# A graph network's attention units: the last column block of the probabilities turned by VectorE and the DMA queues in place of TensorE

## The chip, the cores and the metric

The kernel runs on one core of one Trainium2 chip. The metric is the device time of one execution in microseconds. The kernel before took 2339.39 us, the median of three runs (2338.75 to 2340.38). The profile comes from a further execution of 2340.76 us.

## The reference

A batch of 32 graphs with 512 nodes and 64 features each passes through four layers. All four share one 512 x 512 adjacency matrix, symmetric and scaled on both sides by the root of the node's degree. Each layer normalises its input, applies a ReLU, computes an update and adds it to the input. The first three layers are a neighbour sum, two plain graph convolutions, and an additive attention. The fourth, in which most of the time is spent, has eight heads of dot-product attention and an output attention over what the heads produce:

```python
def gat_layer(x, graph, W, b):
    h = x @ W
    s = jnp.einsum('bnd,bmd->bnm', h, h) * graph
    s = jnp.where(s == 0.0, NEG_INF, s)
    a = jax.nn.softmax(s, axis=2)
    return jnp.einsum('bnm,bmd->bnd', a, h) + b
heads = jax.vmap(lambda W, b: gat_layer(flow_x, graph, W, b))(Wh, bh)
...
x = jax.nn.leaky_relu(cat, negative_slope=0.01)
out = gat_layer(x, graph, W_out, b_out)
return jax.nn.leaky_relu(out, negative_slope=0.01)
```

For every graph this is nine attentions with a 512 x 512 score matrix each: scores, a masked softmax along the rows, and the product of the probabilities with the values.

## The kernel before

The file holds two forms: a general one (L1133 on), which did not run here, and the fast one (`fast_form`, L23), which did. All data are float32. With P = 128 partitions, N = 512 nodes make C = 4 row blocks and 4 column blocks.

**Two stages.** The first stage (L756 to L1105) computes the first three layers, for pairs of graphs. The second stage (L1110 to L1129), from about 470 us to the end, computes the fourth layer. The change lies in the second, apart from the helper that prepares the heads' features.

**Units.** The second stage is a row of 144 units. A unit is a pair of attentions that lie in the two halves of the 128 partitions (`halves(k)`, L206, k = 0 or 1, 64 rows each). A `Heads` unit (L457) is two heads of one graph, four such units for each graph, 128 in all. An `Out` unit (L549) is the output attention of two graphs, 16 in all. Both derive from `Pair` (L313).

**Slots.** Time is cut into slots of which each unit starts four, one for each row block r; the next unit starts in the fifth. `planned` (L649) makes a function `slot(k)` (L665), which emits what each unit does in slot k; `at(k, off, span)` (L652) yields the units whose slot number, counted from their own start, is off to off + span - 1, and the step in it. TensorE, VectorE and ScalarE get their instructions exactly in the order in which the code emits them (`manual_schedule`, L121), so the order in `slot` is each engine's queue. Counted from the unit's start, a unit does this:

- Slots -1 to 2: `scores(r)` (L381) on TensorE, two matmuls (k = 0 and 1) into `s_ps`, at the head of the slot. Two `s_ps` tiles exist.
- Slots 0 to 3: `soft(r)` (L357). VectorE adds the mask `flow_neg`, negates and takes the row's extreme in one instruction for each k (L372); ScalarE takes the exponential and the row sum (L365) into `p_att`. Between the second L372 and what follows, the code calls `mid()` (L699), which holds the division of an earlier unit.
- Slots 5 to 8 (`TR` = 5, L299): `transpose(j)` (L391) for column block j = 0 to 3. Sixteen TensorE transposes of 64 x 128 (L399), which alternate between the two row halves of the source, fill two PSUM tiles `pt_ps`; ScalarE copies one of them (L405) and VectorE the other (L407) into `pt_att`. VectorE's copy is emitted after the slot's `soft` and `mid`.
- Slots 6 to 9 (`VA` = 6): `values(j)` (L409). For each k one matmul of 512 columns (L414), accumulated over j in the one tile `av`, which holds the two halves k in the partitions 0 to 63 and 64 to 127.
- Slot 5: `recips()` (L419): VectorE inverts the row sums (L424) and turns them (L426), SP writes them to DRAM (`rec_row`, four small DMAs, L429) and reads them back as a row spread over 64 partitions (`recb`, two DMAs, L434).
- Slot 9 (`END`, L301): `normalize()` (L441), the division: `o_att` = `av` x `recb` (L443), emitted in `mid()`.
- Slots 10 to 13: the heads' weights (`y_ps`, L526), the activation (`cat`, L534 and L311), or for an `Out` unit the bias, a transpose back and the output DMA (L614). The products of an `Out` unit (`gT_ps`, L565) are spread over eight slots before it starts.

In slots where the `y_ps` or `g_ps` matmuls run first (`row_halves`, L499; "led" in the code), the transposes are emitted after the values, otherwise before them.

PSUM: `ps_m` has three tiles with one tag (L1116), which `pt_ps`, `y_ps`, `g_ps`, `gT_ps`, `gV_ps`, `hx_ps` and `back_ps` share.

**What the change touches beside it.** `Heads.prep_late` (L469), six slots before the first unit of a graph: VectorE makes the normalised features `hn` (L474, L475) and the least value for a later test (L478), then GpSimd makes `hs`, the features times `root_d`, once for each k (L483). In the next slot TensorE transposes `hs` into `hx_ps` (L290), and ScalarE copies it (L292). `Out.prep_late` (L580), at the end of the slot two before the unit starts: VectorE makes `gs` = `gT` x `urow` (L583), which the next slot's scores read, and a reduction for the test (L584).

The pools: `wk` has two buffers for each name unless one is given (L1112), `dram` three (L1113), `p_att` and `pt_att` two each.

Of the kernel before, what the change touches and what calls it, by code (L numbers as in the profile page):

```python
# [8 lines left out]
F32 = mybir.dt.float32  # L9
AF = mybir.ActivationFunctionType  # L10
OP = mybir.AluOpType
# [3 lines left out]
P = 128  # L15
# [7 lines left out]
def fast_form(  # L23
# [25 lines left out]
    nc = tc.nc  # L49
    B, N, F = x.shape  # L50
    C = N // P
    H, _, D = w_heads.shape
    G = min(8, B)
    NG = B // G
    F2 = 2 * F

    const = ctx.enter_context(tc.tile_pool(name="const", bufs=1))
    xpool = ctx.enter_context(tc.tile_pool(name="xpool", bufs=1))
# [12 lines left out]
    early = ctx.enter_context(tc.tile_pool(name="early", bufs=1))  # L71
# [17 lines left out]
    def load_blockdiag(src, name):  # L89
        t = setup.tile([P, F2], F32, name=name)  # L90
        nc.vector.memset(t, 0.0)
        for k in range(2):
            nc.gpsimd.dma_start(t[k * F : (k + 1) * F, k * F : (k + 1) * F], src)
        return t
# [19 lines left out]
    for k in range(2):  # L114
        rows = slice(k * F, (k + 1) * F)
# [45 lines left out]
    root_d = const.tile([P, C], F32, name="root_d")  # L161
    urow = const.tile([P, N], F32, name="urow")
# [43 lines left out]
    def halves(k):  # L206
        return slice(k * F, (k + 1) * F)
# [8 lines left out]
    def acc(name, shape):  # L216
        return acc_of[0].tile(shape, F32, name=name, tag=acc_of[1])
# [22 lines left out]
    def gat_weights():  # L240
        pw = acc("wgT_ps", [P, F2])
        nc.tensor.transpose(pw, wg2, ident)
# [56 lines left out]
    TR = C + 1  # L299
# [13 lines left out]
    class Pair:  # L313
# [19 lines left out]
        def prep_late(self, step):  # L333
            pass


        def make_v(self):
            pass


# [40 lines left out]
        def scores(self, r):  # L381
# [3 lines left out]
            for k in range(2):  # L385
# [2 lines left out]
                    start=True, stop=True,  # L388
                )

        def transpose(self, j):  # L391
            pt = pbuf.tile([P, 2, N], F32, name="pt_att", bufs=2)
            self.pts[j] = [pt[:, k] for k in range(2)]

            ps = [ps_m.tile([P, 2, C, F], F32, name="pt_ps", tag="m") for half in range(2)]
            for k in range(2):
                for r in range(C):
                    for half in range(2):
                        nc.tensor.transpose(  # L399
                            ps[half][:, k, r],  # L400
                            self.p[halves(half), k, r, j * P : (j + 1) * P],
                            ident[halves(half), halves(half)],
                        )
            pth = pt.rearrange("p k (r half q) -> p k r half q", r=C, half=2)
            nc.scalar.copy(pth[:, :, :, 0, :], ps[0])  # L405

            return lambda: nc.vector.tensor_copy(pth[:, :, :, 1, :], ps[1])  # L407

        def values(self, j):  # L409
            pt = self.pts.pop(j)  # L410
            if j == 0:
                self.av = ps_v.tile([P, N], F32, name="av")
            for k in range(2):
                nc.tensor.matmul(  # L414
                    self.av[halves(k), :], lhsT=self.v(k, j), rhs=pt[k],
                    start=(j == 0), stop=(j == C - 1),
                )

        def recips(self):  # L419

# [36 lines left out]
    class Heads(Pair):  # L457
# [3 lines left out]
        hs = {}  # L461
# [7 lines left out]
        def prep_late(self, step):  # L469
            b = self.b  # L470
            if step == -2 and self.i == 0:
                mean, rstd = (t[:, b % 2, :, None].to_broadcast([P, C, F]) for t in flow_stats[b // 2])
                h = early.tile([P, C, F], F32, name="hn3", bufs=3)
                nc.vector.tensor_tensor(h, xs[b // G][:, b % G], mean, OP.subtract)  # L474
                nc.vector.scalar_tensor_tensor(  # L475
                    h, h, 0.0, rstd, op0=OP.max, op1=OP.mult
                )
                nc.vector.tensor_reduce(  # L478
                    least[:, b * C : (b + 1) * C], h, AX.X, OP.max
                )  # L480
                hs = early.tile([P, C, 2, F], F32, name="hs3", bufs=2)
                for k in range(2):
                    nc.gpsimd.tensor_tensor(  # L483
                        hs[:, :, k, :], h, root_d[:, :, None].to_broadcast([P, C, F]), OP.mult
                    )
                Heads.hs[b] = hs
                Heads.hn[b] = h

# [60 lines left out]
    class Out(Pair):  # L549
# [23 lines left out]
        def make_v(self):  # L573
# [3 lines left out]
            self.gV = wk.tile([P, C, P], F32, name="gV", bufs=1)  # L577
            nc.scalar.copy(self.gV, ps)

        def prep_late(self, step):  # L580
            if step == 2:
                self.gs = wk.tile([P, N], F32, name="gs", bufs=1)
                nc.vector.tensor_tensor(self.gs, self.gT, urow, OP.mult)  # L583
                nc.vector.tensor_reduce(  # L584
                    least_out[:, self.b // 2 : self.b // 2 + 1], self.gT, AX.X, OP.min,
                    apply_absolute_value=True,
                )
# [61 lines left out]
    def planned(units, products):  # L649
        units = units + [None] * 4  # L650

        def at(k, off, span=C):  # L652

            for u in range(len(units)):
                if units[u] and 0 <= k - u * C - off < span:
                    yield units[u], k - u * C - off

        exps = []

        def led_in(k):  # L660
            for u, j in at(k, -3 * C, 3 * C + END + 5):
                if u.leads(j - 3 * C):
                    yield u, j - 3 * C

        def slot(k):  # L665
            for u, r in at(k, -1):
                u.scores(r)

            led = list(led_in(k))
            for u, off in led:
                u.row_halves(off)

            while exps:
                exps.pop(0)()

            copies = []

            def transposes():  # L680
                for u, j in at(k, TR):
                    copies.append(u.transpose(j))

            if not led:
                transposes()
            for u, j in at(k, VA):
                u.values(j)
            for u, j in at(k, VA - 1, 1):
                u.make_v()
            for n, u in products:  # L690
                u.product(k - n * C)
            for u, j in at(k, -3 * C, 3 * C):
                u.prep_pe(j - 2 * C)
            if led:
                transposes()
            for u, j in at(k, END, 5):
                u.end_pe(j)

            def mid():  # L699
                for u, j in at(k, END, 1):  # L700
                    u.normalize()

            now = list(at(k, 0))
            for u, r in now:
                exps.append(u.soft(r, mid))
            if not list(led_in(k + 1)):
                while exps:
                    exps.pop(0)()
            if not now:
                mid()  # L710
            for copy in copies:
                copy()
            for u, j in at(k, END, 5):
                u.end_late(j)
            for u, j in at(k, TR, 1):
                u.recips()
            for u, j in at(k, -3 * C, 3 * C):
                u.prep_late(j - 2 * C)

        return slot  # L720
# [34 lines left out]
    with (  # L755
# [47 lines left out]
        class Spread:  # L803
# [169 lines left out]
        def slot(k, more):  # L973
# [158 lines left out]
def general_form(  # L1132
# [27 lines left out]
    NG = B // G  # L1160
    F2 = 2 * F

# [66 lines left out]

    wgT2 = const.tile([P, F2], F32, name="wgT2")  # L1230
    bh = const.tile([P, H], F32, name="bh")
# [459 lines left out]
```

## Time and profile before

| | |
|---|---|
| median of three runs | 2339.39 us |
| the profiled execution | 2340.76 us |
| its span in the trace | 2338.9 us |
| mean granted TensorE clock | 0.986 |
| L399 transposes | 9216, 415.6 us busy |
| L405 and L407 copies | 576 each, 582 and 687 ns |
| L414 value matmuls | 2304 passes, 618 to 625 ns each, in overlapping pairs |
| L483 `hs` on GpSimd | 64 instructions of 128 x 256, idle otherwise |
| DMA, whole kernel | 53.11 MB, 23 GB/s on average |

How to read it: "busy" is the time in which at least one instruction of the engine was running, PE is TensorE's matmuls and PEld its weight loads, DVE is VectorE, ACT ScalarE, POOL GpSimd, SP the engine that issues DMAs. A row of instructions names the line of the code, the engine, the tile written and the tiles read (out<-in), the shape and the count, then the busy time and the mean of one. A float32 matmul appears as two passes, each with its own record. The chain of waits is followed back from the last instruction, at each step to what released it. A wait line names who waited, for whom, the microseconds in all, how often and the longest.

### The profile page before, as it was taken

The numbers are of one execution on the slowest core, as the hardware profiler recorded it, in microseconds if no ns is written. First come the engines' busy times: TensorE is split into PE (matmuls) and PEld (weight loads), VectorE is DVE, ScalarE is ACT, GpSimd is POOL, SyncE is SP. The second block draws the span as 40 slices with busy tenths as digits, with TensorE's granted clock in tenths as the row PEclk, the third lists the DMA queues.
The fourth block names the chain that finished last, engine by engine and source line by source line (L and its number), as shares of the span: only waits on it lengthen the run. The fifth ranks groups of instructions, "written<-read, shape, count | busy, mean of one in ns | idle before, by whom it ended". The sixth has DMA issues, their size and how long they took to land.

```text
span 2338.9 us, 49561 instructions
## 1 busy us (share of the span) xinstructions
PE 2248.0 (96%) x19066; PEld 1086.8 (46%) x19066; DVE 1794.3 (77%) x4366; ACT 1576.3 (67%) x3674; POOL 68.4 (3%) x104
## 2 busy tenths in 40 slices
PE   7999998799999999999999999999999999999997
PEld 4676776644444444444444444444444444444443
DVE  6788878677878787878787878787878787878776
ACT  3444433287777777777777777677777777877775
POOL 2000000000000000000000000000000000000000
PEclk9999999599999999999999999999999999999999
DMA  4000000000001000000000000000000000000001
GB/s 125 1 1 1 2 1 1 1 24 20 29 20 29 20 29 19 29 20 29 20 28 20 29 20 29 19 29 20 29 20 28 20 29 20 24 20 24 24 20 39
DMA packets 44645, 53.11 MB, mean 23 GB/s; under 512 B 15928, under 2 KB 25312, under 8 KB 44272
## 3 DMA queue, kind: packets, MB, share of 16 engines
q1 hardware_dynamic: 43888, 49.65, 6.9%
q8 instruction: 152, 2.49, 0.5%
q14 instruction: 93, 0.76, 0.1%
q0 software_dynamic: 512, 0.20, 0.1%
HBM read 43.98 MB, written 4.78 MB: 21 GB/s over the span
## 4 chain that ended last, share of the span: by engine, by line
PE 72%; DVE 4%; POOL 2%; issue 1%; ACT 0%; DMA 0%; SPq 0%; POOLq 0%; DVEq 0%
PE s_ps L386 23%; PE av L414 23%; PE pt_ps L399 13%; PE y_ps L526 5%; PE gT_ps L565 5%; PE g_ps L508 2%; DVE pt_att L407 2%; POOL hs L483 2%; PE hx_ps L290 1%; DVE hn L475 1%; DVE s_att L372 1%; DVE hn L474 0%; DVE gs L583 0%; PE gV_ps L576 0%; PE back_ps L449 0%
## 5 line engine op out<-in xcount | busy, mean ns | idle before, releaser
L365 ACT ACTIVATE p_att<-s_att,negmax 128x512 f32<-128x512 f32 x1152 | 827.7, 723 | 0.0
L372 DVE CUSTOM_DVE_ANT_0 s_att<-s_ps,flow_neg 128x512 f32<-128x512 f32 x1152 | 739.5, 679 | 2.4 <-PE s_ps L386 2.1
L407 DVE COPY pt_att<-pt_ps 128x512 f32<-128x512 f32 x576 | 395.5, 687 | 281.2 <-PE pt_ps L399 226.6
L386 PE MATMUL s_ps<-hx,g 64*128 64x512 f32 x2048 | 570.0, 634 | 5.7 <-DVE negmax L372 5.1
L414 PE MATMUL av<-pt_att,hn 128*64 128x512 f32 x2048 | 552.3, 618 | 0.0
L399 PEld LDWEIGHTS pt_ps<-ident,p_att 64*128 64x128 f32 x9216 | 373.6, 138 | 375.0 <-issue 228.0
L405 ACT COPY pt_att<-pt_ps 128x512 f32<-128x512 f32 x576 | 335.3, 582 | 157.9 <-PE pt_ps L399 152.2
L399 PE MATMUL pt_ps<-ident,p_att 64*128 64x64 f32 x9216 | 415.6, 226 | 2.8 <-DVE pt_att L407 0.9
L534 ACT ACTIVATE cat<-y_ps,bh 128x512 f32<-128x512 f32 x256 | 162.2, 684 | 168.4 <-PE y_ps L526 168.4
L386 PEld LDWEIGHTS s_ps<-hx,g 64*128 64x128 f32 x2048 | 156.1, 187 | 243.6 <-DVE negmax L372 180.6
L365 ACT ACTIVATION_READ_ACCUMULATOR p_att<-s_att,negmax 128x1 f32 x1152 | 224.6, 195 | 0.0
L443 DVE TENSOR_TENSOR o_att<-av,recb 128x512 f32<-128x512 f32 x144 | 99.6, 692 | 140.5 <-PE av L414 139.1
L414 PEld LDWEIGHTS av<-pt_att,hn 128*64 128x64 f32 x2048 | 101.2, 134 | 156.8 <-PE s_ps L386 87.2
L311 DVE SCALAR_TENSOR_TENSOR cat<-cat 128x1024 f32<-128x1024 f32 x128 | 155.5, 1215 | 0.0
L924 PE MATMUL acc<-v,s 64*128 64x65 f32 x2048 | 132.5, 291 | 1.5 <-DVE rec L935 0.8
L924 PEld LDWEIGHTS acc<-v,s 64*128 64x128 f32 x2048 | 129.5, 206 | 6.9 <-issue 2.6
L565 PE MATMUL gT_ps<-cat,wo_sb 128*64 128x512 f32 x512 | 131.7, 593 | 0.0
L526 PE MATMUL y_ps<-o_att,wh_sb 64*128 64x512 f32 x512 | 131.6, 591 | 0.0
L520 ACT COPY g<-g_ps 128x512 f32<-128x512 f32 x128 | 68.8, 589 | 84.2 <-PE g_ps L508 84.2
L833 PE MATMUL nt_ps<-adj_t,hn 128*128 128x512 f32 x256 | 116.2, 597 | 0.8 <-DVE hn L797 0.8
L386 PE MATMUL s_ps<-gs 64*128 64x512 f32 x256 | 72.4, 642 | 24.2 <-DVE gs L583 24.2
L372 DVE DVE_READ_ACCUMULATOR2_ANT negmax<- 128x1 f32 x1152 | 95.3, 83 | 0.0
(166 smaller groups left out, 1571.7 us busy)
## 6 DMA issues: line engine op xcount, KB each, us to landing
recb<-rec_row SPq DMA_DIRECT2D x288, 128.0 KB
rec_row<-rect SPq DMA_DIRECT2D x576, 1.0 KB
out_dram<-y SPq DMA_DIRECT2D x32, 128.0 KB
x<-in_x_dram SPq DMA_DIRECT2D x3, 1024.0 KB
x<-in_x_dram SPq DMA_DIRECT2D x4, 256.0 KB
adj_raw<-in_adj_dram SPq DMA_DIRECT2D x1, 1024.0 KB
mask<-mask SPq DMA_DIRECT2D x4, 256.0 KB
wh_sb<-in_L_gnn_Wh_dram SPq DMA_DIRECT2D x2, 256.0 KB
```

Of the source, the lines that this page charges most:

```text
L311: nc.vector.scalar_tensor_tensor(t, t, 0.01, t, op0=OP.mult, op1=OP.max)
L365: nc.scalar.activation(self.p[:, k, r, :], ns[:, k], AF.Exp, bias=self.negmax[:, k, r : r + 1], scale=-1.0, accum_out=self.sum[:, k, r : r ...
L372: nc.vector.tensor_tensor_reduce(out=ns[:, k], in0=ps[:, k], in1=flow_neg[:, r], scale=-1.0, scalar=BIG, op0=OP.add, op1=OP.min, accum_out ...
L386: nc.tensor.matmul(ps[:, k], lhsT=g[halves(k), r * P : (r + 1) * P], rhs=x[halves(k), :], start=True, stop=True,)
L399: nc.tensor.transpose(ps[half][:, k, r], self.p[halves(half), k, r, j * P : (j + 1) * P], ident[halves(half), halves(half)],)
L405: nc.scalar.copy(pth[:, :, :, 0, :], ps[0])
L407: return lambda: nc.vector.tensor_copy(pth[:, :, :, 1, :], ps[1])
L414: nc.tensor.matmul(self.av[halves(k), :], lhsT=self.v(k, j), rhs=pt[k], start=(j == 0), stop=(j == C - 1),)
L526: nc.tensor.matmul(ps, lhsT=wh_sb[halves(k), h, :], rhs=self.o[halves(k), :], start=True, stop=True,)
L534: nc.scalar.activation(self.cat[:, k], pss[k], AF.Identity, bias=bh[:, h : h + 1], scale=1.0)
L565: nc.tensor.matmul(self.gps[halves(k), :], lhsT=wo_sb[:, h, :], rhs=Heads.cat[b + k, h], start=(h == 0), stop=(h == H - 1),)
L924: nc.tensor.matmul(self.acc[k][:, r], lhsT=self.s[b // 2][halves(k), b % 2, r * P : (r + 1) * P], rhs=self.v[halves(k), b], start=(b == 0) ...
```

## The change

There are four parts.

1. **Column block 3 no longer passes through TensorE.** `transposes()` runs for j = 0 to 2 alone. In its place `turn(r)`, in slots 2 to 5, has VectorE transpose the block in squares of 32 x 32, for both k, in one instruction of 128 x 256 elements for each r; it is emitted in `mid()`, ahead of the division. Every second turn is followed by a DMA from GpSimd that writes 256 KB to a DRAM tile, in pieces of 512 bytes. `route()`, in slot 5 after `recips()`, reads it back with four DMAs of 128 KB, one for each 32 partitions, from GpSimd and SP in turn, so that the squares come to lie where the transposed block has them.
2. **The values of block 3** read this tile directly. As its columns lie in runs of 32, each k takes two matmuls of 256 columns in place of one of 512.
3. **The second copy out of PSUM** is made by ScalarE for blocks 0 and 2, directly after its first; for block 1 it stays with VectorE.
4. **`gs` and `hs`.** `gs` is made in `mid()`, after the turn and ahead of the division, in the same slot as before. `hs` is made by VectorE in one instruction, ahead of the reduction for the test.

```diff
+    Q = P // 32
...
+        def turn(self, r):
+            if r == 0:
+                self.turns = wk.tile([P, Q, C // 2, 2, 2, 32], F32, name="turn")
+                self.rows = dram.tile([P, Q, C // 2, P], F32, name="turn_row")
+            nc.vector.transpose(
+                self.turns[:, :, r // 2, :, r % 2].rearrange("p a k i -> p k a i"),
+                self.p[:, :, r, N - P :].rearrange("p k (a i) -> p k a i", i=32),
+            )
+            if r % 2:
+                nc.gpsimd.dma_start(
+                    self.rows[:, :, r // 2],
+                    self.turns[:, :, r // 2].rearrange("p a k r i -> p a (k r i)"),
+                )
+
+        def route(self):
+            rows = self.rows.rearrange("(b i) a g x -> a i b (g x)", b=Q)
+            pt = wk.tile([P, Q, C // 2, 2, 2, 32], F32, name="turned")
+            for a in range(Q):
+                (nc.sync if a % 2 else nc.gpsimd).dma_start(
+                    pt[a * 32 : (a + 1) * 32].rearrange("p b g k r i -> p b (g k r i)"), rows[a]
+                )
+            self.pts[C - 1] = [
+                pt[:, :, :, k].rearrange("p b g r i -> p g r b i") for k in range(2)
+            ]
...
             nc.scalar.copy(pth[:, :, :, 0, :], ps[0])
+            if j != 1:
+                nc.scalar.copy(pth[:, :, :, 1, :], ps[1])
+                return None
...
             for k in range(2):
-                nc.tensor.matmul(
-                    self.av[halves(k), :], lhsT=self.v(k, j), rhs=pt[k],
-                    start=(j == 0), stop=(j == C - 1),
-                )
+                parts = 2 if j == C - 1 and len(pt[k].shape) > 2 else 1
+                for g in range(parts):
+                    n = N // parts
+                    nc.tensor.matmul(
+                        self.av[halves(k), g * n : (g + 1) * n], lhsT=self.v(k, j),
+                        rhs=pt[k][:, g] if parts > 1 else pt[k],
+                        start=(j == 0), stop=(j == C - 1 and g == parts - 1),
+                    )
...
+                hs = early.tile([P, C, 2, F], F32, name="hs3", bufs=2)
+                nc.vector.tensor_tensor(
+                    hs, h[:, :, None].to_broadcast([P, C, 2, F]),
+                    root_d[:, :, None, None].to_broadcast([P, C, 2, F]), OP.mult,
+                )
                 nc.vector.tensor_reduce(
                     least[:, b * C : (b + 1) * C], h, AX.X, OP.max
                 )
-                hs = early.tile([P, C, 2, F], F32, name="hs3", bufs=2)
-                for k in range(2):
-                    nc.gpsimd.tensor_tensor(
-                        hs[:, :, k, :], h, root_d[:, :, None].to_broadcast([P, C, F]), OP.mult
-                    )
...
+        def make_gs(self):
+            self.gs = wk.tile([P, N], F32, name="gs", bufs=1)
+            nc.vector.tensor_tensor(self.gs, self.gT, urow, OP.mult)
+
         def prep_late(self, step):
             if step == 2:
-                self.gs = wk.tile([P, N], F32, name="gs", bufs=1)
-                nc.vector.tensor_tensor(self.gs, self.gT, urow, OP.mult)
...
             def transposes():
-                for u, j in at(k, TR):
+                for u, j in at(k, TR, C - 1):
                     copies.append(u.transpose(j))
...
             def mid():
+                for u, r in at(k, 2):
+                    u.turn(r)
+                for u, j in at(k, -2, 1):
+                    u.make_gs()
                 for u, j in at(k, END, 1):
                     u.normalize()
...
             for u, j in at(k, TR, 1):
                 u.recips()
+                u.route()
```

More of the change, by code (lines that the diff above doesn't have):

```diff
@@ L338, in make_v @@
             pass
+        def make_gs(self):
+            pass
         def leads(self, off):
@@ L578, in make_v, with make_gs @@
             nc.scalar.copy(self.gV, ps)
+        def make_gs(self):
+            self.gs = wk.tile([P, N], F32, name="gs", bufs=1)
+            nc.vector.tensor_tensor(self.gs, self.gT, urow, OP.mult)
         def prep_late(self, step):
             if step == 2:
-                self.gs = wk.tile([P, N], F32, name="gs", bufs=1)
-                nc.vector.tensor_tensor(self.gs, self.gT, urow, OP.mult)
                 nc.vector.tensor_reduce(
@@ L711, in slot @@
             for copy in copies:
-                copy()
+                if copy:
+                    copy()
             for u, j in at(k, END, 5):
```

## The prediction

> **What bounds the kernel now.** I read the page first (busy shares, the chain that ended last, the costliest groups), then the waits of TensorE, then the chain over 15 us of the steady part, then the DMA issues.
>
> The page's first part and its chain by line:
>
> ```profile
> PE 2248.0 (96%) x19066; PEld 1086.8 (46%) x19066; DVE 1794.3 (77%) x4366; ACT 1576.3 (67%) x3674; POOL 68.4 (3%) x104
> ...
> PE s_ps L386 23%; PE av L414 23%; PE pt_ps L399 13%; PE y_ps L526 5%; PE gT_ps L565 5%; PE g_ps L508 2%; DVE pt_att L407 2%; POOL hs L483 2%; PE hx_ps L290 1%; DVE hn L475 1%; DVE s_att L372 1%; DVE hn L474 0%; DVE gs L583 0%; PE gV_ps L576 0%; PE back_ps L449 0%
> ```
>
> TensorE is busy 96%, and three of its steps (scores, values, transposes) are 59% of the path that sets the end. [...] This is the chain of waits of a short unit, with start, length and step:
>
> ```profile
> 1016.24 1.06 PE s_ps L386 x4
> 1017.29 0.49 PE pt_ps L399 x16
> 1017.79 1.01 PE av L414 x4
> 1018.79 1.06 PE s_ps L386 x4
> 1019.86 0.49 PE pt_ps L399 x16
> 1020.35 1.01 PE av L414 x4
> 1021.36 1.06 PE s_ps L386 x4
> 1022.41 0.86 PE y_ps L526 x4
> ```
>
> Each piece starts where the last one ends: no other engine stands between them, so a step taken off TensorE here shortens the path by its whole length. What still makes TensorE idle is in its waits (us in total, times, longest):
>
> ```profile
> PE s_ps L386 <- DVE gs L583: 24.2, 16, 2.0
> PE hx_ps L290 <- POOL hs L483: 17.6, 32, 4.2
> ...
> PE s_ps L386 <- DVE negmax L372: 5.1, 14, 0.4
> ```
>
> Both upper lines are steps that the diff moves. VectorE and ScalarE have room, but not much: in 500 to 1000 us they are busy 385.91 and 376.22 of 500 us. The intervals between divisions (L443) in the timeline repeat every nine units: 12.2, 11.3, 13.3, 11.3, 14.9, 14.7, 13.7, 13.3, 11.9 us, 12.94 on average. Short units are tighter than the mean.
>
> [...]
> [...] a value group's four passes start at 1006.137, 1006.143, 1006.617 and 1006.623, so both halves run at once. [...] each float32 matmul shows as two passes, and half 1's first pass started before half 0's second.
> [...] those at the start of the kernel land 4.6 to 8 us after issue, but beside loads that kept the DMA engines 99% busy:
>
> ```profile
> wl<-in_L_gnn_net_params_dram POOLq DMA_DIRECT2D x4, 16.0 KB, 7.8
> ...
> wg<-in_L_gnn_W_dram POOLq DMA_DIRECT2D x2, 16.0 KB, 4.8
> ...
> bh_raw<-in_L_gnn_bh_dram POOLq DMA_DIRECT2D x1, 4.0 KB, 4.6
> ```
>
> [...] the trace has only 211 ns for 128x32 (L426)[...].
> [...]
>
> **The change, part by part.** I count against the profiled execution, 2340.8 us (span 2338.9); the median, 2339.4, is 1.4 lower.
>
> 1. **TensorE transposes of block 3** go: 16 per unit, 0.49 us on the path in the excerpt. Where the group stands behind the values it shows 0.65, but then the scores after it show 0.91 in place of 1.06, so the net is again 0.5. 144 x 0.49 = 70.6 us, all on the path.
>
> 2. **Copies out of PSUM.** VectorE loses three of its four copies a unit (3 x 0.69 = 2.06 us); ScalarE gets two more and loses one (+0.58 us). VectorE gets four turns of 128x256: other 256-element rows take 0.414 to 0.425 us, so 4 x 0.42 = 1.68 [...]. VectorE comes out level or a little lighter. ScalarE's short unit becomes 8 exponentials at a pitch of 0.72, 5 copies at 0.57 and 2 of L534 at 0.63, 9.9 us of 10.8. That is 92%, and a second copy now stands before the exponentials, so I charge 10 us (0 to 30) of new waits. Its cover is the slot between transposes and values.
>
> 3. **Turn in front of the division.** In the unit at 1010 us VectorE ended its reductions at about 1009.62 and sat 0.45 us until the values were there (1010.12). The turn of 0.42 fits into that gap: nothing. Where the gap is missing, 0.4 us falls on y's wait, which is hidden as long as y's slot starts with 1.06 us of scores.
>
> 4. **Output units' gs** moves ahead of the copy of block 1, which waits for late transposes in just that slot; a turn of 0.42 stands before it instead. I take 22 of the 24.2 us (at least half goes, at most all).
>
> 5. **hs on VectorE.** Two GpSimd instructions of 1.2 us together become one of 512 elements, 0.69 us, ahead of the least-value reduction. 30 steady waits of 0.44 us, 13 us; I take 11 (0 to 17). It costs VectorE 0.69 us in four units: hidden.
>
> 6. **Values of block 3** are four matmuls of 256 columns in place of two of 512, half 0's pair first. Same columns: nothing, if half 1 may pass half 0's second matmul as it passes its second pass now. If it may not, it starts 0.43 us (half of 0.86) late: 144 x 0.43 = 61 us. Strided 128-byte runs as moving data are not in the trace; I charge nothing. I take 0 as likelier, 61 as the other end.
>
> 7. **The DMA round trip.** GpSimd issues two writes a unit, 512 pieces of 512 bytes each, then two of the four reads (128 pieces of 1 KB); SP issues the other two behind rec_row and recb. Nothing else remains on GpSimd's queue, and on SP only the next unit's row and outputs, which have slots to spare. What waits in the end is TensorE, at the values of block 3, with all later scores queued behind them. The time there is: turn ended at 1010.04, values at 1020.28, so the period less 1.04 us: 9.7 us in the shortest unit after part 1, 11.2 on average. Issue on GpSimd took 0.53 us for 64 pieces and 0.60 to 0.76 for 128, so 1.0 to 2.1 for 512 (estimate). [...] High end, with the 4.6 us of the trace: write 0.1 + 4.6 + 1.5 (more pieces) + 1.1 (256 KB at the 229 GB/s that recb reached), reads 0.7 + 4.6 + 1.0, together 13.6. SP's way: recb's issue ended 5.1 us after the turn, two issues of 0.48, and 768 KB at 229 GB/s: about 9.4. I take 9.4: no stall. At the end of the kernel, slots are shorter: 3 us.
>
> Sum: 2340.8 - 70.6 - 22 - 11 + 10 + 3 = 2250; by the median, **2249 us**.
>
> **Rivals.**
> **The value matmuls of one half run one behind the other (part 6).** For it: [...] that every paired group in the kernel alternates its halves, so no row shows the other order. Against: the passes above do overtake. 2249 + 61 = 2310, with 2285 to 2335 for partial cases and for round trips of 10 to 12 us.
> **The round trip becomes the bound: slower.** The next unit's last turn runs in the very slot where TensorE waits, ahead of that wait, so an overrun costs half: stall = (trip + 1.04 - period)/2. With 13.6 us and the mean period 12.25: 1.2 us x 144 = 172 us, 2421. It eats the 90 us of gain at 0.63 us a unit, so from a trip of about 12.5 us on the kernel is slower. For it: 4.6 us landings, and two in a row. Against: those ran among loads at 99% DMA busy; here the share is 8%.
> **ScalarE becomes the bound.** Its 92% in short units speaks for it; the mean, by the same pitches 95 us of work in nine units that last some 110 after the change, against. All 30 us give 2269: still in the forecast's own range.
>
> **Chances.** Forecast (2225 to 2285): 0.47. Halves in a row or half a stall (2285 to 2335): 0.28. In between, within 0.2% of before: 0.05. Round trip too long (over 2344): 0.20. 0.2% is about what a measurement of this kernel can tell from no change. Range: 2225 leaves out some 0.05 below, 2350 some 0.14 above. Faster 0.75, same 0.05, slower 0.20.
>
> **What would show it.** Right: pt_ps at three quarters of its count; the av groups at about 1 us for block 3 too; the wait of scores on gs and of hx on hs near zero; the turn at about 0.42 us; no wait of av on a DMA. Wrong: av after a DMA high among TensorE's waits (trip), or block 3's value group at 1.3 to 1.5 us (halves in a row), or pt_ps and av waiting on ScalarE's copies by more than 30 us.

## The result, and the profile after

The changed kernel took **2261.68 us**, the median of four runs (2258.63 to 2264.65), against 2339.89 us for the kernel before, run beside it. The ratio is 0.966, with a 95% interval of 0.964 to 0.968: 78 us less. The forecast was 2249. The profiled execution took 2259.57 us, 81 us less than that of the kernel before; its span is 2257.6 us, and the mean granted clock 0.988.

The page's first part and its chain, by engine and by line:

```profile
PE 2167.4 (96%) x17338; PEld 1028.7 (46%) x17338; DVE 1748.1 (77%) x4542; ACT 1634.1 (72%) x3818; POOL 399.4 (18%) x616
...
PE 59%; DVE 16%; issue 3%; DMA 1%; ACT 1%; SPq 0%; POOL 0%; DVEq 0%; POOLq 0%; ACTq 0%
PE s_ps L392 19%; PE av L452 18%; PE pt_ps L430 8%; DVE s_att L378 8%; PE y_ps L565 5%; PE gT_ps L604 5%; DVE pt_att L441 3%; PE g_ps L547 2%; DVE hs L518 1%; DVE turn L401 1%; DVE cat L312 1%; DVE hn L514 1%; DVE hn L513 0%; DVE least L522 0%; DVE least_out L625 0%
```

The busy shares hardly moved, and read alone they say that TensorE is still the bound. The chain says otherwise: VectorE now holds 16% of it, with its masking and reductions (L378) at 8%, where they stood at 1% before. TensorE's waits show the same (us in total, times, longest):

```profile
PE s_ps L392 <- DVE negmax L378: 30.2, 48, 0.7
...
PE hx_ps L291 <- DVE hs L518: 3.3, 1, 3.3
...
PE av L452 <- DMA turned<-turn_row: 1.6, 1, 1.6
```

The wait of the scores on `gs` (24.2 us before) is gone, and that of `hx_ps` on `hs` fell from 17.6 to 3.3. In their place the scores wait for VectorE's reductions, 30.2 us against 5.1. The value matmuls wait once for the round trip, at the end of the kernel.

The groups of the page that belong to the change (busy us, mean ns; then idle time before them and what ended it), and its DMA issues (KB each, us from issue to landing):

```profile
L430 PE MATMUL pt_ps<-ident,p_att 64*128 64x64 f32 x6912 | 312.6, 226 | 1.3 <-ACT pt_att L436 0.6
...
L401 DVE STREAM_TRANSPOSE turn<-p_att 128x256 f32<-128x256 f32 x576 | 253.8, 441 | 18.1 <-ACT p_att L371 17.6
...
L482 DVE TENSOR_TENSOR o_att<-av,recb 128x512 f32<-128x512 f32 x144 | 99.5, 691 | 189.2 <-PE av L452 182.7
L441 DVE COPY pt_att<-pt_ps 128x512 f32<-128x512 f32 x144 | 99.0, 687 | 180.9 <-PE pt_ps L430 180.9
...
turn_row<-turn POOLq DMA_DIRECT2D x288, 256.0 KB, 2.7
...
turned<-turn_row POOLq DMA_DIRECT2D x288, 128.0 KB, 3.0
```

The transposes are three quarters of their count. A turn takes 0.44 us. The copy of block 1 (L441) is the place to look at: VectorE stood idle for 180.9 us ahead of it, 1.26 us a unit. All the other copies have left VectorE, and the one that stayed is the one that comes in a led slot, where the transposes are emitted behind the values. The wait itself isn't new: in the kernel before, VectorE stood idle for 169 us ahead of the same copy. What stands behind it in VectorE's order is late. The chain through one short unit shows what that is:

```profile
962.66 0.69 PE pt_ps L430 x16
963.35 0.02 issue
963.37 0.69 DVE pt_att L441
964.06 0.60 DVE s_att L378
964.66 0.01 DVE negmax L378
964.67 0.60 DVE s_att L378
965.27 0.01 DVE negmax L378
965.28 0.33 DVE turn L401
965.61 1.06 issue
966.66 0.68 DVE s_att L378
967.34 0.01 DVE negmax L378
967.35 0.60 DVE s_att L378
967.96 0.02 DVE negmax L378
967.98 0.04 issue
968.02 1.13 PE s_ps L392 x4
969.15 0.49 PE pt_ps L430 x16
969.64 1.02 PE av L452 x8
```

From the late transposes the path goes into VectorE: the copy, the reductions of this slot, the turn, 1.06 us in which VectorE was busy with the activation (`cat`, L312, 965.56 to 966.74 in the timeline; the chain calls it "issue"), and the reductions of the next slot. Only then is an `s_ps` tile free for the scores. This takes 4.67 us, 0.13 us more than TensorE's own work in that stretch: the value group ahead of these scores starts at 966.88 and takes 1.01 us. The reductions at 964.06 read scores that were there from 960.8 us on, and start only behind the copy.

In the same stretch of the kernel before, the copy and the last reduction were these (VectorE's timeline):

```profile
1013.78 0.69 DVE L407 COPY pt_att<-pt_ps 128x512 f32<-128x512 f32 x1 [0.83 <-PE pt_ps L399]
...
1018.56 0.08 DVE L372 DVE_READ_ACCUMULATOR2_ANT negmax<- 128x1 f32 x1
```

The scores started at 1018.73, 0.09 us after the last reduction. VectorE took 4.86 us from the copy's start to this end, and takes 4.59 us now (963.37 to 967.96), while TensorE lost 0.49 us of transposes. So the two engines were almost level before the change; it took more from TensorE than from VectorE, and VectorE now comes last. In the excerpt of the chain after, the last line is the value group of block 3: eight passes in 1.02 us, as long as the four passes before.

The intervals between divisions (from the timeline, us) say where the gain is. The same nine units, before and after:

```
short  hs     short  gT     gT     gs     hs
11.29  13.28  11.28  14.91  14.73  13.67  13.28  11.87  12.18   sum 116.49
10.95  13.03  10.95  14.19  14.18  12.38  13.03  11.52  11.21   sum 111.44
-0.34  -0.25  -0.33  -0.72  -0.55  -1.29  -0.25  -0.35  -0.97        -5.05
```

Here "hs" marks the two units in which a graph's `hs` is made, "gT" two that hold an output unit's products, and "gs" the unit before an output unit. There are 16 such rounds: 16 x 5.05 = 80.8 us, nearly all of the 81 us between the profiled executions. A short unit gained 0.34 us, not the 0.49 that the transposes took.

### The profile page after: what moved, and what is told of

Read it like the earlier page. It is cut to its first block, busy times and chain, and to the rows that moved or that the text cites. A ratio compares the mean times of both kernels' runs of the same rounds, so it can differ in the third digit from the quotient of the medians.

```text
span 2257.6 us, 47717 instructions
## 1 busy us (share of the span) xinstructions
PE 2167.4 (96%) x17338; PEld 1028.7 (46%) x17338; DVE 1748.1 (77%) x4542; ACT 1634.1 (72%) x3818; POOL 399.4 (18%) x616
## 4 chain that ended last, share of the span: by engine, by line
PE 59%; DVE 16%; issue 3%; DMA 1%; ACT 1%; SPq 0%; POOL 0%; DVEq 0%; POOLq 0%; ACTq 0%
PE s_ps L392 19%; PE av L452 18%; PE pt_ps L430 8%; DVE s_att L378 8%; PE y_ps L565 5%; PE gT_ps L604 5%; DVE pt_att L441 3%; PE g_ps L547 2%; DVE hs L518 1%; DVE turn L401 1%; DVE cat L312 1%; DVE hn L514 1%; DVE hn L513 0%; DVE least L522 0%; DVE least_out L625 0%
## 5 line engine op out<-in xcount | busy, mean ns | idle before, releaser
L378 DVE CUSTOM_DVE_ANT_0 s_att<-s_ps,flow_neg 128x512 f32<-128x512 f32 x1152 | 736.4, 675 | 2.9 <-PE s_ps L392 2.9
L392 PE MATMUL s_ps<-hx,g 64*128 64x512 f32 x2048 | 573.1, 637 | 26.7 <-DVE negmax L378 23.1
L452 PE MATMUL av<-pt_att,hn 128*64 128x512 f32 x1536 | 414.2, 618 | 0.4 <-DVE rec L463 0.4
L406 POOL DMA_DIRECT2D turn_row<-turn x288 | 206.3, 716 | 1167.7 <-DVE turn L401 972.8
L430 PEld LDWEIGHTS pt_ps<-ident,p_att 64*128 64x128 f32 x6912 | 279.6, 138 | 280.6 <-issue 180.0
L436 ACT COPY pt_att<-pt_ps 128x512 f32<-128x512 f32 x432 | 250.6, 580 | 90.4 <-PE pt_ps L430 88.7
L430 PE MATMUL pt_ps<-ident,p_att 64*128 64x64 f32 x6912 | 312.6, 226 | 1.3 <-ACT pt_att L436 0.6
L401 DVE STREAM_TRANSPOSE turn<-p_att 128x256 f32<-128x256 f32 x576 | 253.8, 441 | 18.1 <-ACT p_att L371 17.6
L482 DVE TENSOR_TENSOR o_att<-av,recb 128x512 f32<-128x512 f32 x144 | 99.5, 691 | 189.2 <-PE av L452 182.7
L441 DVE COPY pt_att<-pt_ps 128x512 f32<-128x512 f32 x144 | 99.0, 687 | 180.9 <-PE pt_ps L430 180.9
L415 POOL DMA_DIRECT2D turned<-turn_row x288 | 163.1, 573 | 388.5 <-DMA turn_row<-turn 206.6
L438 ACT COPY pt_att<-pt_ps 128x512 f32<-128x512 f32 x288 | 171.5, 596 | 0.0
L452 PEld LDWEIGHTS av<-pt_att,hn 128*64 128x64 f32 x1536 | 76.0, 134 | 194.2 <-issue 81.9
L312 DVE SCALAR_TENSOR_TENSOR cat<-cat 128x1024 f32<-128x1024 f32 x128 | 151.3, 1182 | 0.0
L452 PE MATMUL av<-turned,hn 128*64 128x256 f32 x1024 | 139.6, 392 | 0.0
```

The lines of the kernel that those rows point to most:

```text
L312: nc.vector.scalar_tensor_tensor(t, t, 0.01, t, op0=OP.mult, op1=OP.max)
L378: nc.vector.tensor_tensor_reduce(out=ns[:, k], in0=ps[:, k], in1=flow_neg[:, r], scale=-1.0, scalar=BIG, op0=OP.add, op1=OP.min, accum_out ...
L392: nc.tensor.matmul(ps[:, k], lhsT=g[halves(k), r * P : (r + 1) * P], rhs=x[halves(k), :], start=True, stop=True,)
L401: nc.vector.transpose(self.turns[:, :, r // 2, :, r % 2].rearrange("p a k i -> p k a i"), self.p[:, :, r, N - P :].rearrange("p k (a i) -> ...
L406: nc.gpsimd.dma_start(self.rows[:, :, r // 2], self.turns[:, :, r // 2].rearrange("p a k r i -> p a (k r i)"),)
L430: nc.tensor.transpose(ps[half][:, k, r], self.p[halves(half), k, r, j * P : (j + 1) * P], ident[halves(half), halves(half)],)
```

## The experiments

**The theory** was that VectorE's queue, and not ScalarE's, had become the second bound: the waits of 30 us and the 16% of the chain, through the copy of block 1 and what follows it. **The rivals**: ScalarE, which the prediction had charged; and that part 4, not part 3, decides. All times are medians; each ratio is to the kernel before, run beside it.

| kernel | us | ratio, 95% interval |
|---|---|---|
| changed | 2261.7 | 0.9661, 0.9642 to 0.9680 |
| no_leaky | 2246.5 | 0.9590, 0.9566 to 0.9614 |
| before_no_leaky | 2339.1 | 0.9986, 0.9978 to 0.9994 |
| copies_act | 2251.4 | 0.9621, 0.9594 to 0.9649 |
| copies_dve | 2314.7 | 0.9888, 0.9864 to 0.9913 |
| part3_alone | 2338.0 | 0.9998, 0.9988 to 1.0008 |
| part4_alone | 2331.5 | 0.9968, 0.9955 to 0.9980 |
| hs_on_pool | 2252.9 | 0.9626, 0.9610 to 0.9643 |
| gs_late | 2276.1 | 0.9727, 0.9707 to 0.9747 |
| copies_act_hs_pool | 2252.6 | 0.9634, 0.9610 to 0.9658 |
| halves_alternate | 2258.1 | 0.9649, 0.9632 to 0.9667 |
| write_twice | 2291.8 | 0.9819, 0.9783 to 0.9855 |
| write_thrice | 2530.1 | 1.0828, 1.0767 to 1.0890 |

### VectorE made lighter: no_leaky and its control

```diff
         def end_late(self, step):
-            if step == 2:
-                leaky(self.cat)
+            pass
```

This leaves the activation of the heads' features out (128 instructions of 1.18 us on VectorE), from the changed kernel and, as a control, from the kernel before.

> The changed kernel without the leaky activation of the heads' cat (VectorE, 1.18 us a unit, at the end of slot 3); that part of the computation is left out. Theory 1: the waits of scores on VectorE's reductions that the change brought (30.2 us against 5.1) come from VectorE's own queue around this instruction. Then they fall below 10 us and the time falls by 20 to 35 us, to 2227 to 2242. Theory 2: they come from ScalarE, which makes one copy more and is late with exponentials and PSUM copies. Then the time stays within 6 us of the changed kernel's 2261.7.

> Control: the kernel before without the same leaky activation (left out of the computation). Theory 1: VectorE bounds nothing there (scores wait for it 5.1 us in all), so the time falls by 0 to 10 us only, to 2330 to 2340. If the kernel before gains 20 us or more as well, VectorE stood in the way already and the waits after the change aren't new.

The changed kernel got 15 us faster, the kernel before some 3 us (ratio 0.9986). So VectorE's work weighs in the changed kernel and did not before. It is less than the 20 to 35 us that the theory asked for, and 22.3 us of waits of the scores on the reductions remain in place of under 10: the activation stands in only some of the late queues. The units say which: the gs unit went from 12.38 to 11.76 us and a short one from 10.95 to 10.82, while the hs units kept their 13.03. VectorE's share of the chain by engine fell from 16% to 6%:

```profile
PE 71%; DVE 6%; DMA 1%; ACT 1%; issue 0%; SPq 0%; DVEq 0%; ACTq 0%
```

A short unit now lasts 10.82 us, close to 11.28 - 0.49 = 10.79: step 1's saving is there in full once VectorE is out of the way.

### Where the second copies go: copies_act, copies_dve, part3_alone

copies_act gives ScalarE the second copy of block 1 as well; copies_dve gives all three to VectorE, as before the change; part3_alone makes part 3 of the change alone, in the kernel before (ScalarE copies blocks 0, 2 and 3).

```diff
-            if j != 1:
+            if True:
                 nc.scalar.copy(pth[:, :, :, 1, :], ps[1])
                 return None
```

> The changed kernel with the second PSUM copy of block 1 on ScalarE as well, so that VectorE makes none. Theory 1 (VectorE's queue brings the new waits; its one copy left waits 1.26 us on average for late transposes): 5 to 20 us faster than 2261.7. Theory 2 (ScalarE): 10 to 30 us slower.

> The changed kernel with all three second copies on VectorE, as before the change. Theory 1: VectorE has 1.4 us more in a unit and scores wait for it: 10 to 40 us slower than 2261.7. Theory 2: ScalarE is relieved of two copies: 5 to 15 us faster.

> The kernel before with part 3 alone: ScalarE makes the second copies of blocks 0, 2 and 3, VectorE that of block 1. If part 3 counts only since the other parts put more on VectorE and less on TensorE, nothing comes of it here, TensorE being the bound: 2330 to 2345. If earlier copies are worth something by themselves (the transposes' PSUM tiles free sooner, values wait less), it is 20 us or more faster.

With the copies on VectorE, 53 of the 78 us are lost, more than the 10 to 40 expected: VectorE is busy 83% and the scores wait for it 138 times. First copies_dve's page and TensorE's waits:

```profile
PE 2171.3 (94%) x17338; PEld 1035.0 (45%) x17338; DVE 1916.9 (83%) x4830; ACT 1502.7 (65%) x3530; POOL 399.6 (17%) x616
```

```profile
PE s_ps L392 <- DVE negmax L378: 82.3, 138, 1.1
```

Part 3 alone, in the kernel before, gave nothing (within 0.1%). By unit this is a gain and a loss: the last unit of the round went from 12.18 to 11.73 us, the first gT unit from 14.91 to 15.26. So the copies are not a gain in themselves. They make room for the turns on VectorE, and without this room most of what TensorE saves is lost in VectorE's queue.

With all second copies on ScalarE the kernel takes 2251.4 us, about 10 less than the changed one. The scores' wait on the reductions falls to 1.2 us, and on the chain ScalarE takes VectorE's place:

```profile
PE 62%; ACT 16%; issue 1%; DVE 1%; DMA 0%; SPq 0%; DVEq 0%; ACTq 0%
```

Its short units last 10.97 us, no less than the changed kernel's 10.95; the gain comes from the hs units (13.03 to 12.52) and the gs unit (12.38 to 11.81), while the two gT units lose (14.19 to 14.59 each). There TensorE's transposes wait for the second of ScalarE's copies to free a PSUM tile (32 waits of 0.2 us, 6.9 us in all, and a chain through L436 and L438). So each engine becomes the second bound when it makes this copy: the theory holds for the changed kernel, the rival for copies_act.

### Part 4 taken apart: part4_alone, gs_late, hs_on_pool, copies_act_hs_pool

part4_alone is the kernel before with both moves of part 4. The other three take one of them back:

```diff
             def mid():
                 for u, r in at(k, 2):
                     u.turn(r)
-                for u, j in at(k, -2, 1):
-                    u.make_gs()
...
             if step == 2:
+                self.make_gs()
```

```diff
-                hs = early.tile([P, C, 2, F], F32, name="hs3", bufs=2)
-                nc.vector.tensor_tensor(
-                    hs, h[:, :, None].to_broadcast([P, C, 2, F]),
-                    root_d[:, :, None, None].to_broadcast([P, C, 2, F]), OP.mult,
-                )
                 nc.vector.tensor_reduce(
                     least[:, b * C : (b + 1) * C], h, AX.X, OP.max
                 )
+                hs = early.tile([P, C, 2, F], F32, name="hs3", bufs=2)
+                for k in range(2):
+                    nc.gpsimd.tensor_tensor(
+                        hs[:, :, k, :], h, root_d[:, :, None].to_broadcast([P, C, F]), OP.mult
+                    )
```

> The kernel before with part 4 alone: gs ahead of the division, hs on VectorE in one instruction. By the prediction's steps 4 and 5 it saves 22 + 11 = 33 us: 2306, with the waits of scores on gs and of hx on hs near zero. Rival: the waits only go to other steps, since VectorE's queue stays as long as it was: 2325 to 2340.

> The changed kernel with gs made at the end of the slot again; all else as changed. Theory 1: gs ahead of the division is the useful part of part 4, with about 1 us for each of 16 output units (measured in part 4 alone: 1.03 us an interval): 16 us slower, 2272 to 2282 us, with 18 to 25 us of waits of the scores on gs. Theory 2 (as VectorE's lateness sets that slot in the changed kernel, the place of gs only swaps one wait for another): within 4 us of 2261.7.

> The changed kernel with hs made by GpSimd again, in two instructions behind the least-value reduction; all else as changed. Theory 1 (VectorE's queue decides: in part 4 alone, hs on VectorE lengthened the units that hold it by 0.33 us, and there are 64 such instructions, two of them for each graph): the 17.6 us wait of hx_ps on hs comes back, but some 44 us of VectorE work leave its queue; the two cancel or it is faster, 2250 to 2262 us (the changed kernel had 2261.7), with the wait of the scores on the negated reductions below 28 us. Theory 2 (as predicted: VectorE hides hs): 11 us slower, about 2272, the scores' wait on the reductions still about 30 us.

> All second copies on ScalarE and hs on GpSimd; all else as changed. Theory 1 (VectorE's queue is what is left): with the copies on ScalarE the wait of the scores on the reductions is gone already (2251.4 us), so taking hs off VectorE brings back the wait of hx_ps on hs and gains nothing: 2251 to 2262. Rival (hs in VectorE's queue still lengthens the units around it, without a wait that TensorE shows): 5 to 10 us faster, 2241 to 2246.

Part 4 alone gained 7 us where the prediction had counted 33. The wait on `gs` is gone from its list and that of `hx_ps` on `hs` is down to its first, 3.3 us, and the wait of the scores on VectorE stands there in their place (5.1 us before):

```profile
PE s_ps L389 <- DVE negmax L375: 33.6, 59, 0.8
```

By unit, the gs unit went from 13.67 to 12.64 us and the two hs units from 13.28 to 13.61. So 16 x (2 x 0.33 - 1.03) = -5.9 us: `gs` ahead is a gain of 16, `hs` on VectorE a loss of 11.

In the changed kernel it is the same. gs_late is 14.5 us slower, and its list has the wait on `gs` back (23.1 us). hs_on_pool is about 9 us **faster** (2252.9, with a range of 2252.26 to 2253.48 over five runs), though the wait that part 4 had taken away is back as well:

```profile
PE hx_ps L291 <- POOL hs L522: 14.8, 32, 4.2
...
PE s_ps L392 <- DVE negmax L378: 8.2, 16, 0.6
```

The wait, 0.34 us a graph apart from the first, is more than repaid: with it, the hs units last 12.67 us in place of 13.03. (The change makes `hs` in one instruction for each of the 32 graphs, 22 us of VectorE in all, not in 64 with 44 us, as the expectation has it.) The chain of the changed kernel shows why. In the led slot of an hs unit VectorE makes `hn`, `hs` and the least value between the late copy and its reductions:

```profile
974.32 0.69 DVE pt_att L441
975.01 0.34 DVE hn L513
975.35 0.02 issue
975.37 0.43 DVE hn L514
975.81 0.02 issue
975.83 0.69 DVE hs L518
976.52 0.33 DVE least L522
976.85 0.60 DVE s_att L378
...
978.12 1.13 PE s_ps L392 x4
```

All 0.69 us of `hs` lie on the path that ends in the scores, once in each of these units. With the copies on ScalarE this chain is broken elsewhere, so taking `hs` back to GpSimd adds nothing there: copies_act_hs_pool, at 2252.6, is the same as copies_act (their intervals overlap). Three versions thus beat the changed kernel by about 9 to 10 us, and the two edits don't add up.

### The halves: halves_alternate

```diff
-            for k in range(2):
-                parts = 2 if j == C - 1 and len(pt[k].shape) > 2 else 1
-                for g in range(parts):
+            parts = 2 if j == C - 1 and len(pt[0].shape) > 2 else 1
+            for g in range(parts):
+                for k in range(2):
```

> The changed kernel with the four matmuls of block 3's values ordered by column half first and then by k, so that the halves of the partitions alternate. As predicted (half 1 passes half 0's second matmul anyhow): no difference, within 4 us of 2261.7, and the group of eight passes stays at 1.02 us. Rival (start in strict order, hidden so far by a slack elsewhere): the group gets shorter by up to 0.4 us and the kernel faster by 20 to 60 us.

2258.1 us: the interval holds the changed kernel's ratio, and every unit's interval is within 0.03 us of the changed kernel's. The order of the four matmuls doesn't matter. In the changed kernel's order the trace has both halves side by side: the eight passes of one group start in pairs 0.01 us apart (969.571 and 969.585, 969.838 and 969.851, 970.054 and 970.067, 970.270 and 970.283).

### The round trip made longer: write_twice, write_thrice

The second write of a unit is issued twice or three times, into the same place; the values are unchanged.

```diff
-                nc.gpsimd.dma_start(
-                    self.rows[:, :, r // 2],
-                    self.turns[:, :, r // 2].rearrange("p a k r i -> p a (k r i)"),
-                )
+                for again in range(3 if r == C - 1 else 1):
+                    nc.gpsimd.dma_start(
+                        self.rows[:, :, r // 2],
+                        self.turns[:, :, r // 2].rearrange("p a k r i -> p a (k r i)"),
+                    )
```

> The changed kernel with the second write to DRAM made twice, one after the other: the trip from the last turn's end to the landed block grows from 7.2 us by about 2.9 us to 10.1. The time until values need it is the period less 1.04 us, 9.9 us in the shortest unit. By the prediction's step 7: no stall worth naming, 2255 to 2270.

> The same write made three times: a trip of about 13 us, above the 12.5 us from which the prediction has the change lose. Its formula, stall = (trip + 1.04 - period)/2 with the period at 12.37 us, gives 0.83 us a unit, 120 us: 2380. If an overrun costs its whole length and not half of it: 240 us, 2500. If TensorE hides it otherwise: near 2262.

In the changed kernel the trace has GpSimd's reads issued 3.6 and 4.2 us (median) after the last turn's end, and landing 3.0 us later. From each last turn's end to the landing of GpSimd's second read it is 7.3 us in the median. SP's reads have no landing in the trace, but where the values waited in write_twice and write_thrice, they mostly started 0.1 us after GpSimd's second read had landed, so this is the trip that counts. The DMA engines' busy share over the second stage, 0.08 before, is 0.36. The values started 12.7 us after the turn in the median, and under 10.87 in four units only, near the kernel's start and end. With two writes the reads are issued at 6.7 and 7.3 us, and the trip is 11.2 in the median and 10.1 to 12.9 over the units, longer than the 10.1 expected. 34 of the 144 units wait, and the kernel loses 30 us: more than expected, with 26.6 us of waits ahead of the values. With three, the reads are issued at 10.6 and 11.2 us, the trip is 14.7 (expected: 13), and the kernel takes 2530 us, above what either price had given. TensorE's waits in it:

```profile
PE av L453 <- DMA turned<-turn_row: 192.4, 86, 7.4
```

This is 1.3 us a unit, while the time from turn to values grew by 3.26 us in the mean (12.46 to 15.72): the wait does come to a little under half of the overrun, as the prediction had argued. With the trip as it was, its formula gives (14.7 + 1.04 - 12.37)/2 = 1.68 us a unit, 243 us, for 197 us of waits (192.4, and 5.9 that the list calls "issue", less the 1.6 of the changed kernel). But the wait is not the whole price. The mean granted clock fell from 0.988 to 0.955, which over the two spans is (1 - 0.955) x 2530.6 - (1 - 0.988) x 2257.6 = 87 us of full clock more, at most, as some of it may have been granted while TensorE stood idle. One stall, in the timeline:

```profile
999.33 1.09 PE L453 MATMUL av<-turned,hn 128*64 128x256 f32 x8 [3.25 <-DMA turned<-turn_row]
1000.35 2.08 PE L392 MATMUL s_ps<-gs 64*128 64x512 f32 x4
1002.22 1.81 PE L566 MATMUL y_ps<-o_att,wh_sb 64*128 64x512 f32 x4
1003.96 1.08 PE L453 MATMUL av<-pt_att,hn 128*64 128x512 f32 x4
```

After 3.25 us of idling, the four score passes take 2.08 us in place of 1.13, and the next matmuls 1.81 in place of 1.04. 197 us of waits and up to 87 us of clock make at most 284; between the profiled executions it is 273, between the medians 268.

## Why the prediction was right, and where it was not

The forecast of 2249 was 13 us too low, and its direction, main mechanism and range held. That it came so close is in part luck, as two errors in the sum partly cancel.

- **Step 1 (transposes, -70.6)** held. Gone from TensorE are a quarter of the transposes; with VectorE out of the way a short unit shows -0.46 us (no_leaky), against the 0.49 charged.
- **Step 2 (copies, +10, with ScalarE as the cause)** named the wrong engine. VectorE's load was counted right, since it came out lighter, but a load is not a queue: the copy of block 1 makes VectorE wait 180.9 us for late transposes, and what stands behind it then is late, with 0.09 us to spare before the change in the unit shown. ScalarE's copies gained more than they cost: without two of them, 53 us are lost, because the turns need the room. This was argued nowhere: the step asked whether VectorE was lighter, not where in its order the remaining copy stood.
- **Step 3 (turn ahead of the division, 0)** held: VectorE still waits for TensorE ahead of nearly every division (182.7 us, 141 of 144 times).
- **Step 4 (`gs`, -22)** gave 14.5 us (gs_late): the wait on `gs` went, and a part of it came back as a wait on the reductions (22.5 us in gs_late, 30.2 in the changed kernel), since the copy, the turn, the activation and the reductions behind it are late in that slot. "At least half goes" was right, the value taken too high.
- **Step 5 (`hs`, -11)** is the step that failed: it had the wrong sign. `hs` on VectorE costs about 9 us in the changed kernel (hs_on_pool) and 11 in the one before (part4_alone, by the intervals). "It costs VectorE 0.69 us in four units: hidden" took VectorE's idle time for cover. That idle time lies ahead of the copy and the division, not in front of the scores.
- **Step 6 (values in halves, 0)** held: 1.02 us for eight passes in the changed kernel, and units within 0.03 us of it in the other order (halves_alternate). The late start of half 1 that the prediction weighed against it, 0.43 us, is not what the trace shows: half 1's passes start 0.01 us apart from those of half 0's two matmuls, which stand ahead of it in the program.
- **Step 7 (round trip, 9.4 us, no stall; +3 at the end)** held in that nothing stalled: 7.3 us by GpSimd's reads, and 1.6 us of waits at the end. The 9.4 was SP's way, whose landing the trace doesn't show. The write landed 2.7 us after its issue and GpSimd's reads after 3.0, where the high end of 13.6 had 4.6 for each before it added anything for their size. The landings of 4.6 us and more among the loads at the kernel's start (DMA engines 99% busy, 36% in the second stage now) had been too high for an end of the range.

The total by experiments: part 4 gave -14.5 + 8.8 = -5.7 us, not -33. That leaves -78.2 + 5.7 = -72.5 for all the rest (not run alone, so this takes the parts to add up), where steps 1, 2 and 7 had -57.6. The prediction was 27 us too hopeful on part 4 and 15 too careful on the rest. By unit, three gained more than the 0.49 of step 1: the two gT units 0.72 and 0.55, and the last of the round 0.97, of which part 3 alone gives 0.45. Parts 1 and 2 without the others were not run.

The **rivals**: halves in a row did not occur. The round trip has 10.87 us at its tightest in the steady part and takes 7.3 in the median, so it isn't the bound. Its price for 10 to 12 us, 2285 to 2335, fits write_twice (11.2 us, 2291.8). For longer trips it was too low: at 14.7 us the formula gives 243 us, 268 were measured, and what it left out is the clock. The break-even at 12.5 us lies between the two and was not tried. ScalarE as the bound came true only for copies_act, where it stands at 16% of the chain and the kernel is faster for it.

What stays open is which order would free the led slot altogether; no version without the late copy on either engine was run.

## What to carry to other kernels

When one engine is relieved, look in the second engine's queue for the instruction that waits longest, and count everything behind it up to the next thing that the first engine needs: VectorE's load fell, and yet taking the one copy that stayed off it gained 10 us. Ask as well how much time the second engine had to spare at that point; here it was 0.09 us in the unit shown, behind a TensorE that was busy 96%. Idle time covers a moved instruction only if it lies between that instruction and the waiter (`hs`, 0.69 us a graph, cost about 9 us with VectorE busy 77%); a removed wait on the list isn't a gain until the interval of the unit shrinks (part 4 alone: 38.5 us of waits gone, 7 us gained). And a step off the path may need a second step that is worth nothing alone (here the copies: 0 us by themselves, 53 beside the turns).

## What the hardware showed beside it

In write_thrice the stalls cost more than their length: 197 us of waits, 273 us of time between the profiled executions. The first matmul group that follows block 3's values after a stall ran at its usual speed in all 44 cases where the stall was under 1.9 us, but clearly slower, mostly at half speed, in 26 of 40 between 1.9 and 3.16 us and in all 13 above. In the stall shown above, of 3.25 us, the scores' four passes took 2.08 us against 1.13.

The granted clock in the same trace shows which stalls cost more. It has two values, 1 and 0.5, and changes on a grid of 3.41 us. The traces of the changed kernel and the kernel before show the grid as well: stretches at half clock of 10.24, 6.83 and 27.31 us (3, 2 and 8 steps) in the one, up to its last, and one of 3.41 us, near its end, in the other. These are three steps of the grid around the stall above:

```profile
core 0: us, PE busy (x) PEld busy (x) DVE busy (x) ACT busy (x) POOL busy (x), PEclk, DMA share, GB/s
993.56:996.97 3.41, 1.97 (x22) 0.96 (x20) 2.76 (x10) 2.57 (x8) 1.77 (x4) 1.00 0.67 190
996.97:1000.39 3.42, 1.06 (x10) 0.63 (x10) 0.00 (x0) 0.93 (x3) 0.36 (x1) 1.00 0.62 194
1000.39:1003.80 3.41, 3.41 (x9) 1.14 (x8) 2.56 (x8) 0.00 (x0) 1.00 (x2) 0.50 0.27 78
```

From 470 to 2470 us, half clock came after the 37 steps at full clock in which TensorE was busy for 44.0% or less, that is idle for 1.9 us or more, and after none of the 502 with 44.4% or more. The first step above has 1.97 us of work and the clock stays; the second has 1.06 and it is halved. So in this stretch a stall of 2 to 3 us cost clock only where it left TensorE idle for 1.9 us or more of one step. In the first stage, where other matmuls run, a step with more busy time than this was followed by half clock too (1.84 of 3.41 us, 54%, in the kernel before, from 411.73 us on), so the share isn't a rule for every kernel. In the changed kernel the granted clock of the second stage is 1 up to 2247.38 us, 10.22 us before its end.

The transposes of 128 x 256 on VectorE, read and written in runs of 32, took 0.44 us each, against 0.41 to 0.42 us for VectorE's other rows of 256 elements (L513, L514, L522). GpSimd's issue of a write of 512 pieces took 0.72 us, that of a read of 128 pieces 0.57.
